# Preparing the embedding's weights: all even terms first, in four PSUM banks, with the first samples' load moved ahead of the odd terms

## The chip, the cores and the metric

The kernel runs on one core of a Trainium2 chip. The metric is the device time of one execution in microseconds; the time before is the median of three runs. A core has five engines with instruction queues of their own: TensorE (PE; its weight loads are listed apart as PEld), VectorE (DVE), ScalarE (ACT), GpSimd (POOL) and SyncE (SP), which here issues most transfers. Each engine works off its own list of instructions in order; engines wait for one another, and for transfers, at semaphores.

## The reference, cut to what matters

A tower of a patch embedding, one attention-like layer and a mixture of experts, on 4 x 64 x 512 x 64 samples. The change touches the first step alone, the embedding:

```python
xp = jnp.pad(x, ((0, 0), (0, 0), (0, PAD), (0, 0)), mode='edge')
patches = xp[:, :, idx, :]                      # patches of 16 samples, 8 apart
patches = jnp.transpose(patches, (0, 4, 2, 3, 1))
xf = jnp.fft.rfft(patches, axis=-2, norm='ortho')
x_emb = jnp.concatenate([x_real, x_imag], axis=-1)
x_emb = x_emb @ W.T                             # to 256 features
```

It is followed by a layer norm, the layer with a decaying scan over time and an MLP, another norm, and eight experts of which each token uses two. A Fourier transform followed by a matrix is one matrix, so the kernel folds both into one set of weights before it starts on the samples.

## The kernel before, in words

The tokens are worked on in 32 blocks of 512 (128 rows by four). A block is embedded, passes the layer and the router, and its tokens are then given to the experts in tiles of 256. Three blocks are in work at a time. For most of the kernel (from `tc.manual_schedule` on) the order of the instructions on PE, DVE, ACT and SP is written out by hand. Ahead of that, in the set-up, the framework's scheduler orders each engine's instructions, and it may mix them with the first operations of the hand-written part.

The set-up makes the embedding's weights `wu` (five combinations, four parts `j`, 256 features):

- SP issues, in this order: the Fourier coefficients `cf` (L116), the token weights `wf` in three pieces (L120: the first even term, the other three even terms, the four odd terms), and the samples of the first block, `xb` (L121, through `load_x`, L106). Then follow the weights of the layer (L153 to L170) and later the samples of the second block, into the same single buffer.
- DVE makes `same` from the identity matrix (L124), and from it and `cf` the left operands `mix`, one piece for each `j` (L128).
- PE multiplies `mix` by `wf` (L139): for each `j` four even terms are summed in one half of a PSUM bank and four odd terms in the other half. The banks come from the pool `p_mm` (name `mm`, two banks).
- ACT copies each finished bank to `wu` (L146); DVE derives three further combinations from it (L148 to L150).

The first block's samples are turned into differences `xv` by nine operations of DVE (`differences`, L401 and L398), six of which read `xb`. The embedding (L426) multiplies `xv` by `wu`, in three groups, each in a bank of the pool `p_tm` (name `tm`, three banks); ACT (L435) and DVE (L432) take them up. PE then does small products (L239, `fold`) that move the norms' offsets into the biases; they need columns that POOL prepares after it has converted the table `rc_f` (L171). After the norm (POOL L299 to L304, DVE L308) PE transposes the block (L321) and multiplies it by the layer's weights (L369).

## Time and profile before

| | us |
|---|---|
| median of 3 runs (lowest, highest) | 2064.63 (2062.04, 2065.77) |
| the profiled execution, its own time | 2063.66 |
| its span from first to last instruction | 2061.9 |
| PE busy | 2029.4 (98% of the span) |
| DVE busy | 1731.6 (84%) |
| ACT busy | 1180.6 (57%) |
| POOL busy | 1015.2 (49%) |
| PE's products of the weights (L139), first start | 3.92 |
| the embedding's first product (L426), start | 23.17 |
| mean granted clock of PE | 0.996 |

The profile shows one execution. Times in it are counted from the start of the span. A row of the timeline gives the start, the length of the merged run, the engine, the line, the operation with its tiles and shapes, how many instructions it merges, and in brackets how long the engine had been idle and which work released it. Every f32 product is listed as two passes, so that a line with 32 products shows 64. The granted clock is the share of full speed at which PE was allowed to run.

### The profile page before, as it was taken

The page shows a single profiled execution, that of the slowest core. Times are in us where ns is not written, and L with a number is a line of the kernel's source. Part 1 is how long each engine was busy: PE and PEld are TensorE (multiplying, and loading weights), DVE is VectorE, ACT ScalarE, POOL GpSimd, SP SyncE. Part 2 cuts the span into 40 slices and gives each one's busy share as a digit, 9 for nine tenths or more (in the row PEclk, how much of TensorE's full clock was granted, in tenths as well). Part 3 has the DMA queues.
Part 4 walks back from the last instruction along what each step waited for, and adds up shares of the span by engine and source line. Part 5 has one row for each costly group of instructions (what it writes and reads, how often), then busy time and mean ns, then how long its engine had stood idle before and what let it go on. Part 6 is the DMA issues. An engine that isn't in the chain of part 4 may idle for free.

```text
span 2061.9 us, 32343 instructions
## 1 busy us (share of the span) xinstructions
PE 2029.4 (98%) x9618; PEld 1684.4 (82%) x9618; DVE 1731.6 (84%) x5100; ACT 1180.6 (57%) x2325; POOL 1015.2 (49%) x925
## 2 busy tenths in 40 slices
PE   8999999999999999999999999999999999999997
PEld 6777777888888888888888888888888888866775
DVE  6777878998999989999999989999989899967554
ACT  2344455566666766666667666566766666645442
POOL 2133344455555545555555455555555555545544
PEclk9999999999999999999999999999999999999999
DMA  4031256666776667667776776677667667697643
GB/s 145 1 109 62 88 132 138 132 156 148 158 165 147 153 135 161 146 146 164 154 155 141 148 153 147 159 162 155 149 138 160 147 145 165 132 245 153 86 65 51
DMA packets 424529, 283.33 MB, mean 137 GB/s; under 512 B 355104, under 2 KB 391072, under 8 KB 420256
## 3 DMA queue, kind: packets, MB, share of 16 engines
q1 hardware_dynamic: 373424, 208.35, 43.4%
q0 software_dynamic: 49632, 67.39, 17.7%
q10 hardware_dynamic: 1296, 5.52, 0.9%
q8 instruction: 76, 1.25, 0.3%
q14 instruction: 101, 0.83, 0.1%
HBM read 118.36 MB, written 86.52 MB: 99 GB/s over the span
## 4 chain that ended last, share of the span: by engine, by line
PE 90%; DVE 4%; DMA 1%; issue 1%; POOL 0%; ACT 0%; SPq 0%; POOLq 0%; DVEq 0%; ACTq 0%
PE tm L731 21%; PE tm L426 12%; PE tm L1118 10%; PE mm L1101 10%; PE sums L567 8%; PE sums L691 7%; PE sums L369 6%; PE mm L691 4%; PE mm L582 2%; PE tm L691 1%; PE mm L1183 1%; PE tm L1200 1%; PE mm L589 1%; PE mm L583 1%; PE tm L651 1%; PE tm L807 1%
## 5 line engine op out<-in xcount | busy, mean ns | idle before, releaser
L1147 POOL DMA_INDIRECT out<-y,xg x226 | 371.4, 1643 | 326.7 <-DVE y L1137 233.9
L731 PE MATMUL tm<-w_sb,aT 128*128 128x256 f32 x2048 | 454.8, 380 | 0.2 <-DVE z L654 0.2
L731 PEld LDWEIGHTS tm<-w_sb,aT 128*128 128x128 f32 x2048 | 386.6, 190 | 57.8 <-DVE z L654 5.4
L913 POOL DMA_INDIRECT xbuf<-row,to x248 | 252.7, 1019 | 151.3 <-DVE ks L603 85.9
L426 PE MATMUL tm<-wu,xv 128*128 128x256 f32 x1280 | 290.3, 379 | 0.0
L426 PEld LDWEIGHTS tm<-wu,xv 128*128 128x128 f32 x1280 | 242.7, 190 | 32.7
L1101 PE MATMUL mm<-xT,w 128*128 128x256 f32 x1008 | 240.3, 381 | 4.4 <-ACT xT L1094 4.4
L1118 PE MATMUL tm<-w,ge 128*128 128x256 f32 x1008 | 240.7, 382 | 0.0
L342 ACT COPY planes<-zz 128x1024 uint16<-128x1024 uint16 x75 | 75.9, 1044 | 272.6 <-DVE zz L308 264.2
L1101 PEld LDWEIGHTS mm<-xT,w 128*128 128x128 f32 x1008 | 191.8, 191 | 34.7 <-ACT xT L1094 5.3
L1118 PEld LDWEIGHTS tm<-w,ge 128*128 128x128 f32 x1008 | 189.4, 190 | 30.5 <-issue 2.2
L299 POOL TENSOR_SCALAR rstd<-mv 128x4 f32<-128x4 f32 x62 | 41.6, 671 | 319.8 <-DVE mv L280 295.4
L1094 ACT COPY xT<-xh 128x512 uint16<-128x512 uint16 x262 | 181.6, 764 | 7.5 <-DMA xh<-xbuf 7.3
L1109 ACT ACTIVATE ge<-mm,w 128x256 f32<-128x256 f32 x252 | 105.3, 470 | 139.2 <-PE mm L1101 128.4
L1135 DVE TENSOR_TENSOR y<-tm,w 128x512 f32<-128x512 f32 x126 | 86.8, 689 | 53.9 <-PE tm L1118 45.3
L369 PE MATMUL sums<-hT,w_sb 128*128 128x512 f32 x256 | 112.8, 592 | 0.0
L401 DVE TENSOR_TENSOR xv<-xb 128x512 f32<-128x512 f32 x160 | 106.4, 698 | 4.8 <-DMA xb<-in_x 4.8
L279 DVE BATCH_NORM_STATS2 st<-h 128x6 f32<-128x256 f32 x256 | 105.0, 410 | 3.3
L468 POOL TENSOR_TENSOR h<-h,mb_sb 128x1024 f32<-128x1024 f32 x32 | 76.4, 2386 | 61.2 <-ACT xT L1094 26.0
L369 PEld LDWEIGHTS sums<-hT,w_sb 128*128 128x128 f32 x256 | 48.2, 190 | 53.2 <-issue 52.4
L1137 DVE TENSOR_SCALAR y<-y,tile_share 128x256 f32<-128x256 f32 x262 | 87.6, 376 | 4.6
L435 ACT COPY ab<-tm 128x512 f32<-128x512 f32 x32 | 18.8, 586 | 126.8 <-PE tm L426 126.8
(278 smaller groups left out, 4242.2 us busy)
## 6 DMA issues: line engine op xcount, KB each, us to landing
w<-in_wex SPq DMA_DIRECT2D x112, 641.5 KB, 6.6
xb<-in_x SPq DMA_DIRECT2D x32, 1040.0 KB
out<-h SPq DMA_DIRECT2D x31, 512.0 KB
bank<-in_wex ACTq DMA_DIRECT2D x8, 641.5 KB, 8.8
xbuf<-row,to POOLq DMA_INDIRECT x248, 3.4
out<-y,xg POOLq DMA_INDIRECT x226, 5.9
xh<-xbuf SPq DMA_TRANSPOSE x131, 5.1
xg<-xbuf SPq DMA_DIRECT2D x131, 4.0 KB, 2.5
```

The source lines that it names most:

```text
L369: nc.tensor.matmul(ps, lhsT=w[:, k, ts(m, P)], rhs=rhs[:, k, :], start=k == 0, stop=k == KD - 1)
L401: nc.vector.tensor_tensor(to, a, b, ALU.subtract)
L426: nc.tensor.matmul(ps[:, n, :], lhsT=xv[:, i, j, :], rhs=wu[:, i, j, :], start=j == 0, stop=j == J - 1)
L567: nc.tensor.matmul(g[:, n, :], lhsT=lhsT, rhs=rhs, start=False, stop=True, skip_group_check=True)
L691: nc.tensor.matmul(dst, lhsT=lhsT, rhs=rhs, start=start, stop=True, skip_group_check=True)
L731: last_product[0] = nc.tensor.matmul(ps[:, i, :], lhsT=self.aT[:, k, ts(u * 2 + i, P)], rhs=w2_sb[:, k, :], start=k == 0, stop=k == KH - 1,)
L913: write = nc.gpsimd.indirect_dma_start(out=xbuf, out_offset=bass.IndirectOffsetOnAxis(ap=self.to[:, c, t : t + 1], axis=0), in_=self.row[: ...
L1094: nc.scalar.copy(halves[:, :, :, 1 - i], self.xh[:, i * KD : (i + 1) * KD, :])
L1101: nc.tensor.matmul(ps[:, m, :], lhsT=self.w[:, k * D + m * P : k * D + (m + 1) * P], rhs=self.xT[:, k, :], start=k == 0, stop=k == KD - 1,)
L1109: nc.scalar.activation(self.ge[:, m, :], ps[:, m, :], AF.Gelu, bias=self.w[:, 5 * D + m : 5 * D + m + 1])
L1118: last_product[0] = nc.tensor.matmul(ps[:, c, :], lhsT=self.ge[:, k, ts(c, P)], rhs=w[:, (2 + k) * D : (3 + k) * D], start=k == 0, stop=k ...
L1147: add = nc.gpsimd.indirect_dma_start(out=out, out_offset=bass.IndirectOffsetOnAxis(ap=number[:, c, :], axis=0), in_=y[:, c, :], in_offset= ...
```

## The change

The loop that issues the pieces of `wf` now loads the first block's samples just before the odd terms. The products are looped the other way round: for all four `j` the even terms, then for all four `j` the odd terms. As four sums are open at once, four banks are taken, two from `p_mm` and two from `p_tm`. ACT's copy and DVE's three operations follow each `j`'s odd terms.

```diff
         wf = prep.tile([P, 2, CH, D], F32)
+        xs = {}
         for lo, hi in ((0, 1), (1, CH), (CH, 2 * CH)):
+            if lo == CH:
+                xs[0] = load_x(0)
             to = wf.rearrange("p o k d -> p (o k) d")[:, lo:hi]
             nc.sync.dma_start(out=to, in_=wtok[:, lo:hi, :])
-        xs = {0: load_x(0)}
-
         same = prep.tile([P, C], F32)
...
-        for j in range(J):
-            ps = p_mm.tile([P, 2, D], F32, name="mm")
-            for odd in range(2):
+        banks = [(p_mm, "mm"), (p_mm, "mm"), (p_tm, "tm"), (p_tm, "tm")]
+        pss = [pool.tile([P, 2, D], F32, name=name) for pool, name in banks]
+        for odd in range(2):
+            for j in range(J):
+                ps = pss[j]
                 for k in range(CH):
                     n = (odd * CH + k) * 2
                     nc.tensor.matmul(
...
-            nc.scalar.copy(wu[:, 1:3, j, :], ps)
-            E_j, O_j = wu[:, 1, j, :], wu[:, 2, j, :]
...
+                if not odd:
+                    continue
+                nc.scalar.copy(wu[:, 1:3, j, :], ps)
+                E_j, O_j = wu[:, 1, j, :], wu[:, 2, j, :]
```

The three operations of DVE that follow the copy are unchanged, one level further in. After the change the file is five lines longer from here on: L426 of before is L431 of after, L401 is L406, L139 is L142.

More of the change, by code (lines that the diff above doesn't have):

```diff
@@ L145, in vit_tower_kernel @@
                     )
-            nc.scalar.copy(wu[:, 1:3, j, :], ps)
-            E_j, O_j = wu[:, 1, j, :], wu[:, 2, j, :]
-            nc.vector.scalar_tensor_tensor(wu[:, 3, j, :], E_j, 3.0, O_j, ALU.mult, ALU.subtract)
-            nc.vector.tensor_tensor(wu[:, 0, j, :], E_j, O_j, ALU.add)
-            nc.vector.tensor_tensor(wu[:, 4, j, :], E_j, O_j, ALU.subtract)
+                if not odd:
+                    continue
+                nc.scalar.copy(wu[:, 1:3, j, :], ps)
+                E_j, O_j = wu[:, 1, j, :], wu[:, 2, j, :]
+                nc.vector.scalar_tensor_tensor(wu[:, 3, j, :], E_j, 3.0, O_j, ALU.mult, ALU.subtract)
+                nc.vector.tensor_tensor(wu[:, 0, j, :], E_j, O_j, ALU.add)
+                nc.vector.tensor_tensor(wu[:, 4, j, :], E_j, O_j, ALU.subtract)
     vec = const.tile([P, vecs.shape[1]], F32)
```

## The prediction

> **What bounds the kernel now.** I read the page first: busy shares and the chain that ended last. Both name TensorE (PE).

> ```profile
> PE 2029.4 (98%) x9618; PEld 1684.4 (82%) x9618; DVE 1731.6 (84%) x5100; ACT 1180.6 (57%) x2325; POOL 1015.2 (49%) x925
> ...
> PE 90%; DVE 4%; DMA 1%; issue 1%; POOL 0%; ACT 0%; SPq 0%; POOLq 0%; DVEq 0%; ACTq 0%
> ```

> PE is idle for 2061.9 - 2029.4 = 32 us in all, so a late start of PE is not made up later: nothing after it waits for anything but its own predecessors. The change lies in the first 24 us, so the second view is the timeline of PE there (start, length, instruction, and in brackets the idle time before it).

> ```profile
> 1.83 1.97 PE L102 MATMUL mm<-ident 128*128 128x128 f32 x8 [1.83 <-POOL ident masks.py:199]
> 3.92 1.19 PE L139 MATMUL mm<-wf,mix 128*128 128x256 f32 x2
> 5.29 2.93 PE L139 MATMUL mm<-wf,mix 128*128 128x256 f32 x6 [0.18 <-DMA wf<-in_wtok]
> 9.55 13.78 PE L139 MATMUL mm<-wf,mix 128*128 128x256 f32 x56 [1.33 <-DMA wf<-in_wtok]
> 23.17 8.80 PE L426 MATMUL tm<-wu,xv 128*128 128x256 f32 x40
> ```

> The 32 products of L139 are 64 passes here (each f32 product counts twice). The even terms of j = 0 run early (8 passes); PE then stands 1.33 us until the odd terms have landed (9.55), does the other 56 in one run, and begins the first embedding (L426) at 23.17. Third, the timeline of VectorE (DVE):

> ```profile
> 1.81 0.22 DVE L124 TENSOR_TENSOR same<-ident 128x64 f32<-128x64 f32 x1 [1.81 <-POOL ident masks.py:199]
> 2.60 4.63 DVE L128 TENSOR_TENSOR mix<-cf,same 128x1024 f32<-128x1024 f32 x4 [0.57 <-DMA cf<-in_coef]
> 12.03 1.29 DVE L401 TENSOR_TENSOR xv<-xb 128x512 f32<-128x512 f32 x2 [4.80 <-DMA xb<-in_x]
> ```

> The left operands of L139, `mix`, are ready by 7.23, long before most are used. Then DVE sleeps 4.80 us for the samples `xb`, which land at 12.0. Last, the granted clock (columns: stretch, its length, busy us of PE, PEld, DVE, ACT, POOL, then PEclk, DMA share, GB/s):

> ```profile
> 36.36:43.19 6.83, 5.60 (x12) 2.99 (x13) 5.96 (x13) 3.35 (x7) 1.36 (x2) 0.50 0.00 1
> 43.19:47.00 3.81, 3.81 (x10) 1.71 (x9) 3.78 (x3) 0.69 (x1) 2.19 (x1) 1.00 0.09 11
> ```

> After 3.96 us without a matmul (33.6 to 37.59) PE has half its clock until 43.19, although it is at work from 37.59: 5.6 us. The start is the same: the trace has no clock record before 12.47, but passes of L139 start 0.43 us apart until 12.27 and 0.2156 us apart from then on; after the stop that ended at 9.55, PE was slow for 2.9 us.

> **The change, part by part.** The diff moves one transfer and the order of the products. The built program shows a third move: outside the hand-written order a scheduler places DVE's instructions, and with `xb` issued earlier it now puts two of its readers ahead of the making of `mix`:

> ```
> L406 xv<-xb          waits for the transfer of xb
> L125 same<-ident
> L406 xv<-xb
> L129 mix<-cf,same    x4
> L403/L406 xv ...     five more, then the twelve wu operations
> ```

> DVE works in this order, so `same`, all of `mix`, and every product on PE wait for the samples.

> *1. The transfers on SP's queue.* Issue order was coef, even term 0, even terms 1 to 3, odd terms, x; now x stands ahead of the odd terms. Nothing else on SP moves ahead. When does x land? Landings are recorded for each of 16 DMA engines. Fifteen had done even terms 1 to 3 by 4.93, the odd ones by 7.96 and x by 10.53; the last did so at 5.25, 9.51 and 12.00, and the semaphore waits for the last. On that engine x took 12.00 - 9.51 = 2.49 us. The odd terms, half the bytes (512 against 1040 KB), would take 1.2 us at this rate but took 4.26: it lost 3.06 us in that stretch of time. If x now meets that loss, it lands at 5.25 + 2.49 + 3.06 = 10.8. If the loss belonged to the odd terms, at 5.25 + 3.0 (the median engine's time for x) = 8.3. If the transfers share the engines instead of following each other, at 12.0 as before. I take 10.8: same engine, same stretch. The odd terms then land near 12.0 (the same sum of bytes as x before), long before PE asks for them.

> *2. DVE.* After 10.8: two xv operations 1.29, `same` 0.22, first `mix` 1.22: the first product's operand is there at 13.5 (11.0 to 14.7). It was there at 3.82. The other three `mix` follow 1.14 us apart, faster than PE uses them (8 passes each, 1.72 us at full clock, 3.4 at half).

> *3. PE.* It keeps its 64 passes: 64 x 0.2156 = 13.8 us at full clock. What the change removes is the stop of 1.33 us and the pauses between 3.92 and 9.55; but the early start goes too: PE now stands from 3.8 to 13.5, and begins at half clock. A slow stretch of c us costs c x (1 - 0.2156/0.43) = 0.5 c. [...] The rows above show 2.9 and 5.6 us. [...] I take the rows' mean, 4.3: 13.8 + 2.1 = 15.9 us (15.2 to 16.6). The products end, and L426 starts, at 13.5 + 15.9 = 29.4 instead of 23.17: **+6.2 us**. So the reordering of terms, which was to fill a wait of 1.33 us, has no wait left to fill.

> *4. Banks, ACT, and the weights' derivation.* Two of the four banks now come from the pool `tm` (three banks), so the embedding's second and third groups take banks that ACT (L146) must have copied out. The copies come after each j's odd terms, 1.72 us apart, 0.59 us each; the second group starts 16 passes = 3.4 us after the last product, so the last copy is done 2.8 us before: nothing (uncovered, up to 0.6). DVE's three wu operations per j take 1.1 us, inside the 1.72; the last end 0.6 + 1.1 = 1.7 us after the products, needed at 3.4. Nothing.

> *5. What else is late.* The last read of `xb` by xv ends six operations, some 3.9 us, after `mix` (10.8 + 1.3 + 0.2 + 4.6 = 17.0), at 21, and xv itself 0.7 later, before L426 needs it at 29.4. The read frees `xb`, so SP issues the second x near 21 instead of 18.21; it is first read at 38.5 + 6.2. Queued behind it on SP is the table `rc_f`, which waits for PE's last product anyway (issued 23.36); POOL waits for it, then prepares the fold by 27.0, 4.9 us ahead of PE's L239 at 31.89. All of these move by the same 6.2, so the margin stays. From 23.17 on, the built orders of all engines are equal, and no transfer there is due at an absolute time; I found nothing to absorb the shift.

> *Sum.* The profiled execution took 2063.66 us around its span of 2061.9; it becomes 2069.9. It lay 0.97 below the median of the runs (2064.63). Against the median: 2064.63 + 6.2 = **2070.8 us**, +0.30%. The runs before spread from 2062.04 to 2065.77, so about 0.2%, 4.1 us, is what a measurement can tell from no change.

> **The rivals.**

> *x lands early and the clock opens soon.* Fifteen of sixteen engines speak for it. Landing 8.3 and c = 2.9: 11.0 + 15.2 = 26.2, +3.0 us: 2067.6, within 0.2%. Against it: the slow engine was already last in the three transfers before (2.50, 3.68, 5.25).

> *Not slower: the later stop of the clock falls away.* The half clock from 36.36 to 43.19 costs 5.6 x 0.5 = 2.8 us [...]. The change shifts that stop by 6.2 us. If it is no longer noticed, +6.2 - 2.8 = +3.4: 2068.0, within 0.2%. It decides as soon as the slow stretch shrinks by 4.2 us (2.1 us of time). Against it: the stop's length stays, and some of the runs in the median may have had that luck already.

> *The change does what it says.* Were `mix` still made at 2.60, PE could take all even terms from 5.29 while the odd ones travel. Half clock until about 9, then full: 32 even passes (two of them done by 5.3) end near 13.6, after the odd terms' landing at 12.0; 32 more at 0.2156 end at 20.5: -2.7 us, 2061.9. Against it stands DVE's built order; a scheduler's estimate of the transfer does not move an instruction on the chip.

> **How the numbers follow.** Forecast 0.78, early x 0.10, lost stop 0.08, as it says 0.04. Slower by over 0.2% takes 0.76 of the first and 0.02 of each of the next two: 0.80. Faster by over 0.2% is only the lucky half of the last: 0.02. The rest, 0.18, is no change to be measured. Range: at the low end +3.0 with the lower half of the runs' spread (1.3), at the high end x at 12.0 and c = 5.6, +7.4 + 0.7 = +8.1, with 1.3: 2066.3 to 2074.0.

> **What would show it.** Timeline of DVE after: its first instruction is L406, idle until the landing of x near 10.8, then `mix` from about 12.3 to 17. Timeline of PE: idle from 3.8 to 13.5 with a release by DVE `mix`, 64 passes without a stop, the first 10 or so 0.43 us apart; L431 at 29.4. Waits: DVE for `xb` about 10 us instead of 4.8, no wait of PE for `wf`. Wrong if x lands before 9, if `mix` starts before x, or if the gaps from 23 us on are shorter than before.

## The result, and the profile after

The change makes the kernel slower by a third of a per cent. Over 21 runs each, the median is 2068.78 us after the change (2064.04 to 2073.0) and 2060.88 us before (2058.8 to 2068.01). The ratio is 1.0033, which is +6.8 us, with a 95% interval from 1.0026 to 1.0041, or 5.4 to 8.4 us; the two medians differ by 7.9. The forecast was +6.2 us and 2070.8.

The page of the changed kernel (busy us and share of each engine; then the chain that ended last):

```profile
PE 2030.4 (98%) x9618; PEld 1686.1 (82%) x9618; DVE 1732.6 (84%) x5100; ACT 1181.5 (57%) x2325; POOL 1015.6 (49%) x925
...
PE 92%; DVE 4%; issue 1%; DMA 1%; another core or an unknown queue 0%; ACT 0%; POOL 0%; DVEq 0%; ACTq 0%; POOLq 0%
```

PE still bounds the kernel, with about the busy time that it had. The span grew from 2061.9 to 2067.9, so PE is idle for 37.5 us instead of 32.5. Where, the timeline of PE says:

```profile
1.83 1.97 PE L102 MATMUL mm<-ident 128*128 128x128 f32 x8 [1.83 <-POOL ident masks.py:199]
12.08 6.15 PE L142 MATMUL mm<-wf,mix 128*128 128x256 f32 x16 [8.28 <-DVE mix L129]
18.06 3.62 PE L142 MATMUL tm<-wf,mix 128*128 128x256 f32 x16
21.51 3.62 PE L142 MATMUL mm<-wf,mix 128*128 128x256 f32 x16
24.97 3.62 PE L142 MATMUL tm<-wf,mix 128*128 128x256 f32 x16
```

The short stops for `wf` are gone: 64 passes follow each other. In their place stands one stop of 8.28 us, and what ends it is `mix`. The first group of 16 passes takes 6.15 us, the next three 3.62 each: half clock again (0.43 us from pass to pass until 16.9, 0.216 from 17.2 on). The timeline of VectorE names the cause:

```profile
9.41 0.69 DVE L406 TENSOR_TENSOR xv<-xb 128x512 f32<-128x512 f32 x1 [9.41 <-DMA xb<-in_x]
10.02 0.22 DVE L125 TENSOR_TENSOR same<-ident 128x64 f32<-128x64 f32 x1
10.16 0.68 DVE L406 TENSOR_TENSOR xv<-xb 128x512 f32<-128x512 f32 x1
10.76 4.62 DVE L129 TENSOR_TENSOR mix<-cf,same 128x1024 f32<-128x1024 f32 x4
```

VectorE's first instruction of the kernel waits for the samples. `same`, which needs nothing but the identity of 1.8, begins at 10.02 (before: 1.81), and `mix` at 10.76 (before: 2.60), although its coefficients landed at 2.5. The embedding starts at 28.42; in the profile before it was 23.17. Behind `mix` the list holds seven more operations of the differences (my listing of the built order said five).

How much of a late start reaches the end? ACT takes up each of the 32 blocks' embedding with one copy. The row gives the start of the first and of the last of them, before and then in two profiles of the changed kernel:

```profile
L435 ACT COPY ab<-tm x32: 585/585/592, 26.8 to 1803.3; 128x512 f32<-128x512 f32 x32
L440 ACT COPY ab<-tm x32: 586/586/592, 32.1 to 1807.7; 128x512 f32<-128x512 f32 x32
L440 ACT COPY ab<-tm x32: 586/587/593, 31.8 to 1807.2; 128x512 f32<-128x512 f32 x32
```

From the first to the last it is 1776.5, 1775.6 and 1775.4 us, and between 1774.9 and 1776.8 in all 13 profiles of this study: up to the last block a late start is handed on nearly whole. What follows varies more. From the last copy to the end of the span it is 258.6, 260.2 and 255.3 us here (255.0 to 260.9 in all), so that two executions of the same kernel differ by 5 us there. The time of one execution therefore does not tell how its start went; the medians do the weighing.

### The profile page after: what moved, and what is told of

Read it like the earlier page. It is cut to its first block, busy times and chain, and to the rows that moved or that the text cites. A ratio compares the mean times of both kernels' runs of the same rounds, so it can differ in the third digit from the quotient of the medians.

```text
span 2067.9 us, 32343 instructions
## 1 busy us (share of the span) xinstructions
PE 2030.4 (98%) x9618; PEld 1686.1 (82%) x9618; DVE 1732.6 (84%) x5100; ACT 1181.5 (57%) x2325; POOL 1015.6 (49%) x925
## 4 chain that ended last, share of the span: by engine, by line
PE 92%; DVE 4%; issue 1%; DMA 1%; another core or an unknown queue 0%; ACT 0%; POOL 0%; DVEq 0%; ACTq 0%; POOLq 0%
PE tm L736 21%; PE tm L431 13%; PE tm L1123 10%; PE mm L1106 10%; PE sums L696 8%; PE sums L572 8%; PE sums L374 6%; PE mm L696 4%; PE mm L587 2%; PE tm L696 1%; PE tm L1205 1%; PE tm L656 1%; PE mm L1188 1%; PE mm L594 1%; PE mm L588 1%; PE tm L812 1%
## 5 line engine op out<-in xcount | busy, mean ns | idle before, releaser
L431 PE MATMUL tm<-wu,xv 128*128 128x256 f32 x1280 | 290.3, 379 | 0.0
L431 PEld LDWEIGHTS tm<-wu,xv 128*128 128x128 f32 x1280 | 242.7, 190 | 32.7
L406 DVE TENSOR_TENSOR xv<-xb 128x512 f32<-128x512 f32 x160 | 106.3, 697 | 9.4 <-DMA xb<-in_x 9.4
```

Of the source, the lines that this page charges most:

```text
L406: nc.vector.tensor_tensor(to, a, b, ALU.subtract)
L431: nc.tensor.matmul(ps[:, n, :], lhsT=xv[:, i, j, :], rhs=wu[:, i, j, :], start=j == 0, stop=j == J - 1)
```

## The experiments

Each kernel was timed beside the kernel before. The table gives what its profile shows of the start, and its ratio to before. "PE from" is the first pass of the products after the last stop over 0.5 us ahead of them, or the first of all where there is none; "embedding" is the start of the embedding's first product.

| kernel | samples land | PE from | embedding | ratio to before (95%) |
|---|---|---|---|---|
| before (first, second, third profile) | 12.0, 11.0, 11.7 | 9.55, 4.04, 9.13 | 23.17, 20.62, 23.70 | 1 |
| changed (first, second profile) | 9.4, 9.3 | 12.08, 11.99 | 28.42, 28.18 | 1.0033 (1.0026 to 1.0041) |
| load moved alone | 9.2 | 11.86 | 28.71 | 1.0033 (1.0020 to 1.0047) |
| load moved further | 6.3 | 11.04 | 27.53 | 1.0026 (1.0018 to 1.0034) |
| changed, PE kept at work | 8.6 | 11.27 | 25.16 | 1.0021 (1.0011 to 1.0032) |
| load moved alone, mix first | 8.6 | 9.93 | 24.87 | 1.0024 (1.0017 to 1.0031) |
| changed, mix first | 9.4 | 4.00 | 19.81 | 0.9995 (0.9987 to 1.0003) |
| the same again | 9.8 | 4.05 | 20.43 | 0.9992 (0.9983 to 1.0000) |
| loop order alone | 10.6 | 4.06 | 18.71 | 1.0002 (0.9994 to 1.0010) |
| changed, mix first, later stop filled | 9.4 | 3.93 | 20.94 | 0.9999 (0.9990 to 1.0007) |

**The order on VectorE undone.** Edges of order, with no wait of their own, are added to the changed kernel: each of the five subtractions that make the first block's differences must stand behind the last making of `mix` in VectorE's list (the helper `placed`, which records such an edge, is left out here):

```diff
...
-            nc.vector.tensor_tensor(
+            last_mix = nc.vector.tensor_tensor(
                 mix[:, j],
...
-                nc.vector.tensor_tensor(to, a, b, ALU.subtract)
+                op = nc.vector.tensor_tensor(to, a, b, ALU.subtract)
+                if self.i == 0:
+                    placed(op, last_mix)
```

Below, this is called the edge.

> The changed kernel, with one edge of order added: the first reader of the samples on VectorE stands behind the last making of mix. Load order, loops and banks stay as changed. Theory (the whole loss is VectorE's order): mix is made from 2.6 to 7.2 again, all even terms run while the odd ones travel, L431's twin (the first embedding product) starts near 20.5, and the time is 8 us below the changed kernel's, 1 to 3 us below before's (ratio 0.9985 to 0.9995). Rival (the loop order, the four banks or the later landing of the odd terms cost something themselves): it stays 3 us or more above before (1.0015 or more).

Measured: 2060.07 us, ratio 0.9995. Timeline of PE, then of VectorE:

```profile
4.00 5.61 PE L150 MATMUL mm<-wf,mix 128*128 128x256 f32 x16 [0.20 <-DVE mix L137]
9.45 3.62 PE L150 MATMUL tm<-wf,mix 128*128 128x256 f32 x16
12.90 3.62 PE L150 MATMUL mm<-wf,mix 128*128 128x256 f32 x16
16.36 3.62 PE L150 MATMUL tm<-wf,mix 128*128 128x256 f32 x16
19.81 8.80 PE L441 MATMUL tm<-wu,xv 128*128 128x256 f32 x40
```

```profile
2.63 4.67 DVE L137 TENSOR_TENSOR mix<-cf,same 128x1024 f32<-128x1024 f32 x4 [0.60 <-DMA cf<-in_coef]
9.43 1.29 DVE L414 TENSOR_TENSOR xv<-xb 128x512 f32<-128x512 f32 x2 [2.13 <-DMA xb<-in_x]
```

Nothing of the diff is undone here, neither the load nor the loops nor the banks, and the whole loss is gone: from 1.0033 to 0.9995. With `mix` made at 2.63 the even terms run while the odd ones travel, and PE has no stop over 0.5 us. So the place of two instructions in VectorE's list is what costs; the rival, that the loops or the later odd terms cost something in themselves in the changed kernel, falls.

**One part of the change at a time.** The kernel before with only the load moved:

```diff
+        xs = {}
         for lo, hi in ((0, 1), (1, CH), (CH, 2 * CH)):
+            if lo == CH:
+                xs[0] = load_x(0)
...
-        xs = {0: load_x(0)}
```

> The kernel before with the load of the first samples moved ahead of the odd terms, and nothing else: products in the old order, two banks. The scheduler's order on VectorE flips as in the changed kernel. Theory: PE waits for mix until about 12, then does 64 passes without a stop, the first embedding product starts at 28 to 29, time 5 to 8 us above before (1.0025 to 1.004), like the changed kernel. Rival (the new loop order is what costs): within 1 us of before.

Measured: 2069.13 us, ratio 1.0033. Timeline of VectorE, then of PE:

```profile
9.19 0.69 DVE L402 TENSOR_TENSOR xv<-xb 128x512 f32<-128x512 f32 x1 [9.19 <-DMA xb<-in_x]
9.80 0.22 DVE L125 TENSOR_TENSOR same<-ident 128x64 f32<-128x64 f32 x1
```

```profile
11.86 17.02 PE L140 MATMUL mm<-wf,mix 128*128 128x256 f32 x64 [8.06 <-DVE mix L129]
28.71 8.80 PE L427 MATMUL tm<-wu,xv 128*128 128x256 f32 x40
```

The move of the load brings the scheduler's other order, the stop and the whole loss, with the old loops. The complement is the changed kernel with the load put back:

```diff
-        xs = {}
         for lo, hi in ((0, 1), (1, CH), (CH, 2 * CH)):
-            if lo == CH:
-                xs[0] = load_x(0)
...
+        xs = {0: load_x(0)}
```

> The changed kernel with the load of the first samples put back behind the odd terms: only the loop order and the four banks are new. VectorE's order is that of before. Theory: even terms run from 5.3 on while the odd ones travel (landing 9.5), no stop of PE, the first embedding product starts near 20.5, time 1 to 3 us below before (0.9985 to 0.9995). Rival (four banks or the new order of sums cost): 1 us or more above before.

Measured: 2062.79 us, ratio 1.0002. Timeline of PE:

```profile
4.06 4.46 PE L141 MATMUL mm<-wf,mix 128*128 128x256 f32 x16 [0.27 <-DVE mix L128]
18.71 8.80 PE L430 MATMUL tm<-wu,xv 128*128 128x256 f32 x40
```

The embedding starts at 18.71, earlier than in any other kernel, as the theory said; of the gain of 1 to 3 us in time nothing is to be seen, nor of the rival's cost of 1 us or more. Neither is shown: the interval, 0.9994 to 1.0010, leaves room from a gain of 1.2 to a cost of 2.1 us.

**The load moved, in the old loops, with mix first.** The load is moved as in the second run, and the edge of the first is added to the kernel before.

> The kernel before with the samples' load moved ahead of the odd terms, and the edge that keeps mix ahead of the samples' readers: old loop order, two banks. Theory: VectorE's order was the whole loss of the moved load, 5 to 8 us; without it only the later landing of the odd terms is left: they land near 10.7, PE stops until then with 56 of 64 passes to do (12.1 us), and the embedding starts at 22.8 to 24.5; time 0 to 3 us above before (1.000 to 1.0015). Rival (the transfer's place itself costs what the changed kernel lost): 5 us or more above before.

Measured: 2066.39 us, ratio 1.0024, which is 4.9 us (1.0017 to 1.0031, or 3.5 to 6.4). This is more than my theory allowed (up to 1.0015) and lies at the edge of its rival (5 us or more). The embedding at 24.87 is a little later than the theory's 22.8 to 24.5. Timeline of PE, then its clock in three stretches (after the length come busy us of PE, PEld, DVE, ACT, POOL, then PEclk, DMA share, GB/s):

```profile
3.91 2.75 PE L148 MATMUL mm<-wf,mix 128*128 128x256 f32 x8
9.93 15.10 PE L148 MATMUL mm<-wf,mix 128*128 128x256 f32 x56 [3.27 <-DMA wf<-in_wtok]
24.87 8.80 PE L437 MATMUL tm<-wu,xv 128*128 128x256 f32 x40
```

```profile
3.90:6.70 2.80, 2.75 (x8) 1.68 (x8) 2.80 (x3) 0.00 (x0) 1.27 (x3) 1.00 1.01 332
8.70:15.50 6.80, 5.57 (x13) 4.50 (x14) 4.95 (x10) 0.58 (x1) 0.00 (x0) 0.50 1.06 377
```

PE waits 3.27 us for the odd terms (from 6.66 to 9.93), and the clock, which had been open (8 passes in 2.75 us), closes at 8.7, when PE has stood for 2.0 us, and stays closed for 6.8 us. So the moved load has a price of its own in the old loops, and this is what the even-first order avoids: with the same load and the same edge the embedding starts at 24.87 in the old loops, at 19.81 and 20.43 in the new ones. The two losses don't add: in the new loops the edge saves 0.4%, in the old ones it brings the ratio from 1.0033 to 1.0024, by less than the noise, as the intervals overlap.

**How much of the loss is the clock.** In the changed kernel PE's 8 transposes at the start are made 64, whose results nobody reads:

```diff
-    for _ in range(2):
+    for _ in range(16):
         ps = p_mm.tile([P, TT, P], F32, name="mm")
```

> The changed kernel, with PE's 8 transposes at the start made 64, so that PE is at work nearly until mix arrives (about 12). It adds work whose result nobody reads. Theory (of the loss of 5 to 8 us, the part beyond the late mix is PE's half clock, 5 us at half speed in the changed kernel): the products then run at full clock from the first pass, L431 starts at 12.1 + 13.8 = 25.9 instead of 28.4, time 2 to 3 us below the changed kernel's. Rival (the clock costs nothing there, or the added passes delay the products): L431 at 28.4 or later, time as the changed kernel's.

Measured: 2063.55 us, ratio 1.0021. Timeline of PE:

```profile
1.83 9.46 PE L102 MATMUL mm<-ident 128*128 128x128 f32 x64 [1.83 <-POOL ident masks.py:199]
11.27 3.69 PE L142 MATMUL mm<-wf,mix 128*128 128x256 f32 x16
14.80 3.62 PE L142 MATMUL tm<-wf,mix 128*128 128x256 f32 x16
...
25.16 8.80 PE L431 MATMUL tm<-wu,xv 128*128 128x256 f32 x40
```

The first 16 passes of the products take 3.69 us instead of 6.15: full clock from the start. The embedding comes 3.3 us earlier than in the changed kernel, 2.5 of it by the clock and 0.8 because the samples landed earlier in this profile. The ratios, 1.0033 and 1.0021, differ by 2.5 us, but their intervals overlap, so the time alone doesn't show it; the trace does. An estimate from both: of the loss of 6.8 us about a third (2.5) is the clock, the rest the late `mix`.

**The later stop filled.** In every profile so far PE has a stop of 3.96 us between the fold and the first block's transposes, and then half clock (a granted clock of 0.50 for 6.83 us in the first profile of before and in that of the changed kernel); I had priced this at 2.8 us. In the kernel with the edge, 32 transposes, unread, fill it:

```diff
...
                     fold(w, g, b, to, room, p_tm.tile([P, 2, D], F32, name="tm"))
+                for _ in range(8):
+                    ps = p_mm.tile([P, TT, P], F32, name="mm")
+                    for t in range(TT):
+                        nc.tensor.transpose(ps[:, t, :], ident, ident)
```

> The changed kernel with mix ahead of the samples' readers (as in the run with that edge alone), and with 32 transposes of the identity put behind the fold's products, where PE stands 3.96 us in every profile so far and then has half its clock. The added work is read by nobody. Theory: the clock stays open, the 3.4 to 6.8 us at half clock behind that stop vanish, and the time falls another 1.5 to 2.8 us: 3 us or so below before (ratio about 0.998 to 0.999), the fastest of all. Rival (the transposes delay the block's own transposes, or the clock closes anyway): as the run with the edge alone, 0.9995.

Measured: 2060.28 us, ratio 0.9999; the time is the rival's, for neither of its reasons. The clock doesn't close, and the block's own transposes begin 14.5 us after the embedding's start, 0.1 us later than with the edge alone. The clock after the stop, first in the kernel with the edge, then in this one:

```profile
34.81:38.22 3.41, 3.41 (x10) 1.95 (x10) 3.34 (x8) 2.25 (x5) 0.00 (x0) 0.50 0.00 0
38.22:42.00 3.78, 3.78 (x10) 1.71 (x9) 3.75 (x4) 1.58 (x3) 2.81 (x1) 1.00 0.00 0
```

```profile
35.10:38.50 3.40, 2.81 (x11) 1.62 (x12) 3.33 (x9) 1.80 (x4) 0.00 (x0) 1.00 0.02 5
38.50:42.00 3.50, 3.50 (x9) 1.52 (x8) 3.46 (x4) 1.82 (x4) 2.18 (x1) 1.00 0.00 0
```

The clock stays open, and yet the way from the first block's embedding to the second's takes 30.51 us instead of 30.62 (20.94 to 51.45, and 19.81 to 50.43). How long the clock is closed there is not always the same: 3.41 us in this profile with the edge alone, 6.83 in the two profiles just named, in which the way takes 31.29 and 30.95 us. In all twelve profiles that have the stop it takes 30.62 to 31.77: up to 1.3 us more than with the stop filled, not 2.8. The columns of the fence say why: in the stretch VectorE is busy for 3.34 of 3.41 us and 3.75 of 3.78. It is making the second block's differences, and then the first block's scan; PE, at half clock or not, waits for it at the end (1.07 us for `ret` with the edge alone, 1.08 with the stop filled).

**The load moved still further.** The samples' load stands ahead of all pieces of `wf`:

```diff
-            if lo == CH:
+            if lo == 0:
                 xs[0] = load_x(0)
```

> The changed kernel with the samples' load moved still further ahead, before all three pieces of wf. The scheduler then puts five of the samples' readers ahead of the last making of mix (four ahead of same) instead of two. Theory: the start of PE is the landing of the samples plus what stands ahead of mix: landing 5.5 to 8, then 3.5 us of readers and same, then 1.2 for the first mix, so PE starts between 10.2 and 12.7 and the embedding between 26 and 29: no better than 2 us below the changed kernel, well above before. Rival (the earlier load helps by its own amount): the samples land 3 us earlier and the time falls by these 3 us.

Measured: 2064.31 us, ratio 1.0026. Timeline of VectorE:

```profile
6.32 1.29 DVE L406 TENSOR_TENSOR xv<-xb 128x512 f32<-128x512 f32 x2 [6.32 <-DMA xb<-in_x]
7.64 0.69 DVE L403 SCALAR_TENSOR_TENSOR xv<-xv 128x512 f32<-128x512 f32 x1
8.37 0.69 DVE L403 SCALAR_TENSOR_TENSOR xv<-xb,xv 128x512 f32<-128x512 f32 x1
8.98 0.22 DVE L125 TENSOR_TENSOR same<-ident 128x64 f32<-128x64 f32 x1
9.12 0.68 DVE L406 TENSOR_TENSOR xv<-xb 128x512 f32<-128x512 f32 x1
9.72 4.62 DVE L129 TENSOR_TENSOR mix<-cf,same 128x1024 f32<-128x1024 f32 x4
```

The samples land 3.1 us earlier than in the changed kernel, PE starts 1.0 us earlier: the scheduler now puts four operations of the differences ahead of `same` and one more ahead of `mix`. In the three places that were tried for this load, the number of these operations ahead of `mix` is none, two and five: the earlier the issue, the more of them.

**The two kernels again, and the best once more.** For further profiles:

> The changed kernel unchanged, for a second profile. Theory: the stop of PE from 3.8 until mix is longer than 8 us, so the products always begin at half clock: again 3.4 to 6.8 us of it, L431 between 27.5 and 29.5. Rival: the clock of the first profile was bad luck, L431 near 26 this time.

> The kernel before, unchanged, for a third profile and as a measure of the method beside the run with the edge. Ratio 1.000; L426 between 20.6 and 23.2 according to when the clock opens (8.0 and 12.5 in the two profiles so far) and when the odd terms land (8.4 and 9.5).

> The changed kernel with the edge alone once more, for a narrower interval and a second profile. Theory: the embedding starts 1 to 3 us earlier than before (19.8 in the first profile, against 20.6 and 23.2 in two profiles of before): ratio 0.9985 to 0.9998. Rival: what is gained at the start is lost again before the end: 1.000.

The kernel with the edge: 2059.77 us, 0.9992 (0.9983 to 1.0000); embedding at 20.43. The changed kernel: 2065.16 us, ratio 1.0033 (1.0020 to 1.0047); embedding at 28.18, 4.7 us of half clock (the first 16 passes took 6.00 us, the next 3.62). The kernel before: 2062.4 us, 1.0003 (0.9995 to 1.0011); embedding at 23.70, a little outside what I had expected, with half clock from 9.13 to about 14 (56 passes in 14.73 us). The second profile of before had this on record:

> The kernel before, unchanged, for a second profile. In the first profile PE's products after the stop ran at half clock until 12.47, and the execution took 2063.66 us, 2.8 us above the median of 21 runs, 2060.88. Theory: before the change PE is at work from 1.83 on but for short stops, so the clock is often open when the stop ends at 9.55; then the products end, and L426 starts, about 1.4 us earlier than in the first profile, near 21.7. Rival: the first profile's start is the usual one, L426 again at 23.2, and the 2.8 us lie later in the kernel. Time against before: ratio 1.000 in both cases.

It gave 2062.44 us, ratio 1.0004 (0.9994 to 1.0014), and this line in the timeline of PE:

```profile
8.43 12.35 PE L139 MATMUL mm<-wf,mix 128*128 128x256 f32 x56 [0.27 <-DMA wf<-in_wtok]
```

56 passes in 12.35 us: the clock was open from 8.0, as the theory had it, and the odd terms had landed 1.1 us earlier than in the first profile, so that L426 started at 20.62. Of the kernel with the edge, both measurements lie below before, but both intervals reach 1; its ratios are the lowest of the study, and still I can't call it faster.

## Why the prediction was right, and where it was not

**The mechanism** was right at each step: VectorE's list begins with a reader of the samples, `mix` and all products wait behind it, the odd terms are never waited for, PE starts at half clock, and the shift of the start is still there at the last block. Undoing the order alone takes the loss away, and bringing it about alone (the load moved, nothing else) produces the same ratio.

**The sum** came out near the measurement (+6.2 against +6.8) with some luck. It is a difference of two starts of the embedding, 29.4 after and 23.17 before, and both were put too late.

*Landing of the samples: 10.8 forecast, 9.4 and 9.3 measured.* I had carried over the whole 3.06 us that the slowest of the 16 DMA engines lost while it moved the odd terms. Less was lost: if the last engine is the same for both transfers, which the landings alone don't show, then after its even terms at 4.96 the samples took it 4.4 us against 2.49 of mere transfer, 1.9 us lost. Over the eight profiles with the load in this place the landing lies between 8.6 and 9.8, so that the sign "x lands before 9" was near (8.6 in two of them). So `mix` and PE were 1.4 us earlier than forecast (12.08 against 13.5).

*The slow stretch of PE: 4.3 us forecast, 5.0 and 4.7 in the two profiles of the changed kernel, 6.0 and 5.3 in those with the load alone and with the load moved further.* The 4.3 was the mean of 2.9 and 5.6; but the 2.9 followed a stop of 1.33 us, the 5.6 one of 3.96, and here the stops were 7.2 to 8.3 us long. The row of 5.6 us in the trace of before was the better guide. What sets the length of a slow stretch, no run showed. The products took 16.3 us (12.08 to 28.42) against 15.9. In all the embedding started at 28.4 and 28.2 instead of 29.4.

*The start before the change: 23.17, taken from the one profile.* Other profiles of the same kernel show 20.62 and 23.70, so the first pass after the stop, the clock and the landing vary from one execution to the next by 3 us. Against 20.62 the changed kernel's 28.3 would be +7.7, against the mean of the three (22.5) +5.8; the measured +5.4 to +8.4 holds both. Which start is the usual one is not shown. A rough estimate: the starts in the eight profiles of the other kernels, each less its measured loss, give 18.3 to 22.2 for it, 20.9 in the mean. Then the start before was put too late by about 2 us, more than the start after.

*The time before: 2064.63, the median of three runs.* The 21 runs of the measurement gave 2060.88; so the forecast of 2070.8 was 2.0 too high, although its shift was too small.

**The rival of the later stop** was priced wrongly. A stretch at half clock was worth 2.8 us only if PE was the bound there. VectorE was for most of it: open or closed, the clock moved the second block by 0.1 us where it was closed for 3.41 us, by 0.8 and 0.4 in two profiles where it was closed for 6.83, and by at most 1.3 in any, and filling the stop brought nothing to be measured. **The rival that the change does what it says** was right in its mechanism, but not in its price: with the edge it happens, the embedding starts near 20, and the time measured is lower by 1.0 and 1.7 us (0.9995, 0.9992), neither of them clear of no change, against the 2.7 that I had worked out from the late start of the first profile. The half clock until about 9 in that sum was an estimate for which I gave no row; with the edge the first 16 passes, from 4.00 on, took 5.61 us and the next 16 took 3.62. **Banks, ACT and the weights' derivation** at nothing: the run with the loops alone agrees within its interval, 1.0002 (0.9994 to 1.0010).

## What to carry to other kernels

Where a scheduler orders the instructions of an in-order engine, moving a load can move its readers too: look up in the built order what now stands behind a wait, because an operation that was ready at 2.6 us may begin at 10.8 through one early reader. Take the starting point of a sum from more than one execution if the stage holds transfers and a clock that opens; here one stage varied by 3 us, half of the effect, and the end of the kernel by 5. And price half clock only in a stretch in which PE is what the others wait for.

## What the runs showed of the hardware

In these two profiles the wait for a transfer ended with the last of its 16 DMA engines: in that of before, fifteen had landed the odd terms by 7.96, the last at 9.51, and PE went on at 9.55; in that of the changed kernel, fourteen had landed the samples by 8.01, the last two at 9.32 and 9.39, and VectorE began at 9.41.
